# A graph network on one core: more edge cells and fewer fetched rows, TensorE's groups in pairs, and a sort without its pads

## The chip, the cores and the metric

The kernel runs on one core of one Trainium2 chip. The metric is the device time of one execution in microseconds (us). An execution is one launch of the whole program; the time given for a kernel is the median of several runs. One more execution is recorded by the hardware profiler, and everything that is said of single instructions comes from that one.

The engines are called by the profile's names: PE (TensorE, matrix products), PEld (its loading of weights), DVE (VectorE), ACT (ScalarE), POOL (GpSimd) and SP (SyncE, which here only issues transfers). POOL issues the indirect transfers, which gather rows of memory by a list of indices.

## The reference: what is computed

A graph has N = 12500 nodes with H = 128 features each and E = 200000 edges (src, dst), sorted by dst. Each edge has 16 attributes and one of 9 types. Four layers follow one another. In each, a node gathers the features of its neighbours, and a small dense network turns the sum into new features:

```python
# layer 0: a message for each edge, summed at dst, then a GRU cell
msg = h[src] @ W_msg.T + b_msg + edge_embed[edge_type]
messages = segment_sum(msg, dst)
x = layernorm(x + gru_cell(messages, x))
# layers 1 to 3 (GIN), summed at src
agg = segment_sum(join(x[dst], edge_attr @ enc_w + enc_b), src)
h = relu(batchnorm(agg @ w1 + b1)) @ w2 + b2
# after layer 3: x = layernorm(x + h)
```

`join` is a sum in layer 1 and a concatenation in layers 2 and 3. The kernel works on sums of features and sums of attributes, and lets the dense part apply the weights to the sums, so what costs time is the gather of 200000 rows by index and their sum by another index, four times.

## The kernel before, in words

**Data.** Nodes are cut into NB = 98 blocks of 128. A feature is kept as three bf16 pieces that add up to the float, so a node's row has H3 = 384 bf16 numbers. The rows of a layer's input lie in SBUF in tiles X of XC = 7 blocks each (14 tiles hold all 98 blocks), and in memory as `table`.

**Cells.** For each pair of an output block o and an input block b there is a cell of SL = 32 slots, which holds up to 32 edges between them (20.8 on average). Four cells are the 128 partitions of one tile of edges. PE gathers such a tile by four matmuls (L1550): a one-hot matrix `g` (128 nodes by 32 slots) picks the rows of block b out of X into PSUM tile `pg`. TG = 3 tiles are a group; `pg` is three PSUM banks wide and has two buffers. ACT copies a group to SBUF as bf16 (`e`, L1559); in layer 0, of every group with an even number k, ACT copies two thirds (L1556) and DVE one (L1557). PE then scatters: a matmul for each tile with the one-hot matrix `s` (128 edges by 128 nodes) adds the edges into the accumulator `acc` (L1507), which has one buffer of one bank.

**Fetched rows.** Layer 0 takes all 98 input blocks as cells: 25 tiles, nine groups. Layers 1 to 3 take only the first `ic` blocks as cells. The edges from the other blocks, and those beyond 32 in a cell, are put in lists, `rt` tiles of 128 edges for each o; POOL fetches their rows from `table` by one indirect transfer for each tile (L1484), and PE scatters them without a gather (L1515). Plan C (layer 1) has ic = 72 and rt = 5: 18 tiles, six groups. Plan D (layers 2 and 3) has ic = 60 and rt = 7: 15 tiles, five groups. Edges that find no place in either are added to memory tables `ovf` by a slow loop ahead of the layer. Fetched rows lie in those X tiles that the layer doesn't need for blocks, one whole X tile for each o; with 3 (layer 1) or 5 such tiles, o's rows are fetched two or four o's ahead.

**The loop** of `layer(i)` runs over o and, within it, over the groups k. Each step issues the gathers of group k, its copy, then the scatters of the group before (with one or two fetched rows), then one piece of other work: a tick of the dense part of a finished pair of blocks (`work`), and the one-hot matrices of the next o (`g` at L1471, four quarters of `s` at L1474). The scheduler may still reorder these within what the data allow. After the last scatter, `finish` adds the three pieces of `acc` into `s` by three DVE additions (L1527 to L1529), and every second o a dense part is queued (`gru` in layer 0, `gin` in the others: transposes L1415, two products L1424 and L1435, all through the one buffer of `psd`).

**Ahead of the layers** the cells' contents must be sorted. Two bitonic sorts of 128×2048 keys run on DVE, B (for attributes and their order) and A (for the cells). `sorter` (L284) runs levels 1 to 16 or 18; an exchange is a min and a max over all 2048 columns, halved between two instructions each (L299 to L322). From level 11 on PE transposes the keys (`turn`) and ACT copies them back. Of the 2048 columns EC = 1600 hold edges; the others hold one pad value. Beside sort B, PE, ACT and DVE count a histogram (`Sizes`).

**Attributes.** For each of the 98 blocks POOL fetches the attributes of its edges by 17 indirect transfers (L736); DVE and ACT prepare them and 17 matmuls add them up (L764). The generator `attributes` gives one step whenever it is asked. Beside sort A it is asked by this loop:

```python
            if at % 6 if at < len(plan) - 20 else done % ATTR:
                next(attr)
                done += 1
```

so at five of six exchanges, until 20 exchanges from the end, and from there only up to the end of a block. What is left is done in layer 0 (`pace`: after groups 1 and 5 of every o, and after group 3 of four o's in five) and in layer 1 (after group 3). When A's keys are stored (L787), POOL gathers the cells' slots in chunks of o's (L791), three of them at once ahead of the listing of the spilled edges, the others within layer 0.

Of the kernel before, what the change touches and what calls it, by code (L numbers as in the profile page):

```python
# [18 lines left out]
H = 128  # L19
# [31 lines left out]
IC = 72  # L51
CELL = 7
PLANS = (Plan("C", IC, 5, False, CELL + IC // 4), Plan("D", 60, CELL, True, 0))
RT = sum(p.rt for p in PLANS)
TW = CELL + IC // 4 + PLANS[0].rt
OV = 8
# [26 lines left out]
assert EP * EC == E and all(p.ic % (4 * TG) == 0 for p in PLANS)  # L83
# [5 lines left out]
def gnn_kernel(ctx: ExitStack, tc: tile.TileContext, x, xT, src, dst, ea, et, w_msg, w_ihT, w_hhT, b_msg,  # L89
# [35 lines left out]
    before = ctile([P, P], "before")  # L125
    V.tensor_scalar(before, diff, 0.0, None, op0=OP.is_gt)
    after = ctile([P, P], "after")
    V.tensor_scalar(after, diff, 0.0, None, op0=OP.is_lt)
    ident = diff
# [154 lines left out]
    def sorter(bufs, end):  # L284

        cur = 0

        def bits(t, c, cd):  # L290
# [4 lines left out]
            if cd == c + 1:  # L295
                v = t.rearrange("p (o r two i) -> p o r two i", two=2, r=2, i=1 << c)
                return [(v[:, :, r, 0, :], v[:, :, r, 1, :]) for r in range(2)]
# [3 lines left out]
        def exchange(c, first, cd, halved=False):  # L301
            nonlocal cur
            n = SC // 2
# [4 lines left out]
            else:  # L308
                exchanged(bufs[cur], bufs[1 - cur], c, first, cd)
# [75 lines left out]
    pre = ExitStack()  # L385
    pst = pre.enter_context(tc.tile_pool(name="pst", bufs=2, space=PSUM))
    pss = pre.enter_context(tc.tile_pool(name="pss", bufs=2, space=PSUM))
    kp = pre.enter_context(tc.tile_pool(name="keysA", bufs=1, side="right"))
# [28 lines left out]
    nc.scalar.dma_start(eti, by_part(et))  # L417
    for k in "BA":
        G.memset(keys[k][0], PADF)
        nc.scalar.dma_start(srt[k][:FRONT].rearrange("(p c) -> p c", p=P), keys[k][0][:, EC:EC + FRONT // P])  # L420
# [10 lines left out]
    def signed(k):  # L431
        odd = keys[k][0].rearrange("p (c two) -> p c two", two=2)[:, :, 1]
# [34 lines left out]
    nidentb = ctile([P, P], "nidentb", BF16)  # L467
# [277 lines left out]
    def add_up(b, at):  # L745
# [24 lines left out]
        yield  # L770
        own6 = owp.tile([P, 6, EA], BF16, name="own6")
        pieces6(own6, own, lambda a, b: own6[:, a:b, :], lambda t, n: t[:, None, :].to_broadcast([P, n, EA]))
        pt = psa.tile([P, 1024], BF16, name="acc") if early else psd.tile([P, 1024], BF16, name="d")
# [138 lines left out]
    class Listed:  # L912
# [24 lines left out]
        def mark(self, ahead):  # L937
# [55 lines left out]
            V.tensor_scalar(c[:, 1:2], self.most[:, 1:2], float(P - 1 - ahead * P), 0.0, op0=OP.add, op1=OP.max)  # L993
# [227 lines left out]
    eap = ctx.enter_context(tc.tile_pool(name="attrs", bufs=4))  # L1221
# [37 lines left out]
    with by_three():  # L1259
# [8 lines left out]
        while at < len(plan):  # L1268
            if at % 6 if at < len(plan) - 20 else done % ATTR:
                next(attr)  # L1270
                done += 1
# [14 lines left out]
        for c in range(3):  # L1286
            slots.gather(c)
        la = Listed()
        listing = la.mark(2)
# [4 lines left out]
        for _ in listing:  # L1294
            pass
    la.rest()
# [6 lines left out]
    ep = ctx.enter_context(tc.tile_pool(name="edges", bufs=3))  # L1303
# [346 lines left out]
```

## Time and profile before

| what | us |
|---|---|
| median of 3 runs | 5772.15 (5763.25 to 5779.61) |
| the profiled execution | 5775.41 |
| its span | 5773.6 |
| PE busy | 4590.5 (80%) |
| POOL busy | 3855.7 (67%) |
| DVE busy | 3500.1 (61%) |
| ACT busy | 3396.2 (59%) |
| weight loads busy | 2754.9 (48%) |

The busy time of an engine is the time in which it ran an instruction; issuing a transfer and waiting don't count. The shares are averages over stages that have different limits, and are to be read stage by stage: the page's second part cuts the span in 40 slices, and the trace can be asked for any stretch, for the waits of an engine in it, and for the timeline of single instructions. In a wait, "PE acc L1515 <- DMA x" means that PE's instruction of line 1515, which writes `acc`, could not start until a transfer into `x` had landed; the numbers behind it are the sum, the count and the longest one, in us. In a group of the page's fifth part the numbers are the busy time in us, the mean of one in ns, and the idle time of that engine just before such instructions with what ended it.

The whole program has 117175 instructions: 45358 matmuls, 9502 of DVE, 4901 of ACT and 3716 of POOL.

### The profile page before, as it was taken

How to read it: one execution, taken by the hardware profiler on the slowest of the kernel's cores; microseconds unless marked ns; L12 is line 12 of the kernel's file. 1: busy time of each engine (PE TensorE's matmuls, PEld its weight loads, DVE VectorE, ACT ScalarE, POOL GpSimd, SP SyncE). 2: the span in 40 equal slices, each digit the busy share in tenths (PEclk: the TensorE clock that was granted, in tenths of full speed). 3: DMA queues.
4: the chain of work that ended last, by engine and by line, in shares of the span. 5: the costliest groups of instructions: out<-in, count | busy, mean ns of one | idle time of the engine just before them, and what ended most of it. 6: DMA issues, size and time to landing. Idle time of an engine off the chain costs nothing. (4 is left out here: it accounts for less than half of the span.)

```text
span 5773.6 us, 117175 instructions
## 1 busy us (share of the span) xinstructions
PE 4590.5 (80%) x45358; PEld 2754.9 (48%) x45358; DVE 3500.1 (61%) x9502; ACT 3396.2 (59%) x4901; POOL 3855.7 (67%) x3716
## 2 busy tenths in 40 slices
PE   3874252118999999999799989988999997999998
PEld 3774122104444444444355555554555554555555
DVE  9987679837887777777444444443444443444444
ACT  7772131106666666666566666665666665666665
POOL 1001878866676767766677777775777776777776
PEclk9755555559999999999899999999999998999999
DMA  5101130012333333323444444445555555555554
GB/s 65 38 1 33 47 90 7 7 35 74 102 89 86 89 89 101 89 85 89 144 128 125 134 121 129 127 115 166 157 160 158 159 155 167 156 156 156 156 157 131
DMA packets 539973, 616.43 MB, mean 107 GB/s; under 512 B 130184, under 2 KB 458028, under 8 KB 538760
## 3 DMA queue, kind: packets, MB, share of 16 engines
q1 hardware_dynamic: 327302, 373.36, 20.1%
q0 software_dynamic: 148192, 202.82, 14.3%
q10 hardware_dynamic: 63914, 32.71, 2.7%
q8 instruction: 355, 5.82, 0.4%
q14 instruction: 210, 1.72, 0.1%
HBM read 519.72 MB, written 88.82 MB: 105 GB/s over the span
## 5 line engine op out<-in xcount | busy, mean ns | idle before, releaser
L1559 ACT CAST e<-g 128x1152 bf16<-128x1152 f32 (+1 forms) x2058 | 2216.2, 1091 | 907.7 <-PE g L1550 766.3
L1484 POOL DMA_INDIRECT x<-table,rowcol x1862 | 1861.2, 1000 | 641.4 <-issue 600.5
L736 POOL DMA_INDIRECT eat<-in_ea,eidcol x1666 | 1794.8, 1077 | 640.0 <-issue 495.0
L1550 PE MATMUL g<-x,g 128*32 128x384 bf16 x28420 | 1688.1, 333 | 93.6 <-DVE e L1557 54.2
L1507 PE MATMUL acc<-e,s 128*128 128x384 bf16 (+2 forms) x7154 | 1646.8, 344 | 116.9 <-ACT e L1556 51.6
L1507 PEld LDWEIGHTS <-s 128*128 128x128 bf16 (+1 forms) x7154 | 939.2, 153 | 745.4 <-issue 470.4
L1550 PEld LDWEIGHTS <-g 128*32 128x32 bf16 x28420 | 613.0, 96 | 911.6 <-issue 711.1
L1474 DVE TENSOR_TENSOR s<-iotas,outcol 128x704 bf16<-128x704 bf16 (+2 forms) x1568 | 838.7, 544 | 0.3 <-PE acc L1507 0.3
L1471 DVE TENSOR_SCALAR g<-inr,pidx 128x1920 bf16<-128x1920 bf16 (+2 forms) x392 | 329.9, 842 | 793.9 <-PE g L1550 685.7
L1515 PE MATMUL acc<-x,s 128*128 128x384 bf16 x1862 | 512.4, 335 | 155.5 <-DMA x<-table,rowcol 153.9
L1556 ACT CAST e<-g 128x768 bf16<-128x768 f32 x392 | 317.2, 809 | 192.9 <-PE g L1550 126.6
L567 PE MATMUL acc<-ot,oa 125*98 125x101 bf16 x1600 | 295.7, 358 | 126.8 <-ACT ot L548 95.6
L1527 DVE TENSOR_TENSOR s<-s,acc 128x128 f32<-128x128 f32 x392 | 112.5, 287 | 408.5 <-PE acc L1507 402.7
L1515 PEld LDWEIGHTS <-s 128*128 128x128 bf16 x1862 | 271.8, 146 | 176.1 <-issue 147.5
L567 PEld LDWEIGHTS <-oa 125*98 125x98 bf16 x1600 | 292.1, 277 | 129.6 <-issue 87.5
L548 ACT ACTIVATE ot<-dbb,bias 125x160 bf16<-125x160 bf16 (+2 forms) x1078 | 332.4, 406 | 16.4 <-PE acc L567 8.2
L800 POOL IOTA num<- 98x2176 uint16 x1 | 1.9, 1947 | 462.4 <-DMA sortedB<-keyB 462.4
L1427 ACT ACTIVATE gates<-d,shift,scale 128x256 f32<-128x256 f32 x294 | 150.1, 561 | 245.7 <-PE d L1425 245.7
L1557 DVE CAST e<-g 128x384 bf16<-128x384 f32 x392 | 216.6, 553 | 75.2 <-ACT e L1556 70.8
L1440 DVE TENSOR_TENSOR n<-d,b 128x256 f32<-128x256 f32 x98 | 41.6, 424 | 279.7 <-PE d L1435 278.6
L764 PEld LDWEIGHTS <-eoh 128*128 128x128 bf16 x1666 | 116.8, 163 | 197.3 <-DVE eoh L758 172.2
L316 DVE TENSOR_TENSOR keyA<-keyA 128x1024 f32<-128x1024 f32 (+1 forms) x178 | 190.9, 1072 | 15.4 <-ACT keyA L332 12.8
(423 smaller groups left out, 4761.8 us busy)
## 6 DMA issues: line engine op xcount, KB each, us to landing
inr<-inrow SPq DMA_DIRECT2D x196, 480.0 KB
inr<-inrow SPq DMA_DIRECT2D x98, 784.0 KB
inr<-inrow SPq DMA_DIRECT2D x98, 576.0 KB
x<-table,rowcol POOLq DMA_INDIRECT x1862
table<-x SPq DMA_DIRECT2D x147, 192.0 KB
eat<-in_ea,eidcol POOLq DMA_INDIRECT x1666
s<-ovf SPq DMA_DIRECT2D x147, 128.0 KB
ovf<-n SPq DMA_DIRECT2D x98, 128.0 KB
```

The lines of the kernel that those rows point to most:

```text
L548: A.activation(self.ot[j % 2][:, b, :ENDS[j] - c0], dbb[:, c0:ENDS[j]], AF.Sign, bias=self.bias[:, b:b + 1], scale=-1.0)
L567: T.matmul(cps[:NB, :NB + NQ - 1], self.oa[c // HC][:, :, c % HC], self.ot[j % 2][:, :, c - (ENDS[j - 1] if j else 0)], start=(c == 0), st ...
L736: G.indirect_dma_start(out=at[:, t, :], out_offset=None, in_=ea, in_offset=bass.IndirectOffsetOnAxis(ap=eidcol[:, b, t:t + 1], axis=0))
L1471: V.tensor_scalar(g[:, :nb * SL], inr[:, :nb * SL], pidx, None, op0=OP.is_equal)
L1474: V.tensor_tensor(st[:, f0:f0 + P // 4, :], iotas[:, f0:f0 + P // 4, :tw], outcol[a][:, o, None, c0:c0 + tw].to_broadcast([P, P // 4, tw]) ...
L1484: G.indirect_dma_start(out=t[:, j, :], out_offset=None, in_=tables[i], in_offset=bass.IndirectOffsetOnAxis(ap=rowcol[:, o, p.kept + j:p.ke ...
L1507: T.matmul(sums[o][:, :wid], st[:m, :, cell + t], e[:m, j, :wid], start=(t == 0), stop=(t == tiles - 1), skip_group_check=True)
L1515: T.matmul(sums[o][:, :H3], st[:, :, row + j], fetched[o][:, j, :], start=False, stop=False, skip_group_check=True)
L1550: T.matmul(pg[c * SL:(c + 1) * SL, j, :H3], g[:, b * SL:(b + 1) * SL], piece(X, b), start=True, stop=True)
L1556: A.copy(e[:, :2, :H3], pg[:, :2, :H3])
L1557: V.tensor_copy(e[:, 2, :H3], pg[:, 2, :H3])
L1559: A.copy(e[:m, :n, :H3], pg[:m, :n, :H3])
```

## The change

**Plans.** IC goes from 72 to 84. Plan C: ic = 84, rt = 3, so 21 tiles and seven groups. Plan D: ic = 72, rt = 5, so 18 tiles and six groups. CELL (where the cells start in the table of columns) 7 to 5, OV 8 to 12. Over the program this makes 31948 gather matmuls of 28420, 8036 scatters of 7154, and 1274 fetches with their matmuls of 1862.

**Rows.** The rows of an o no longer have an X tile of their own; rows fill the spare X tiles as a ring, so four o's have room in each plan and rows are fetched three o's ahead.

**Order in the layers.** PE's order is the one written (`manual_schedule`). Groups are taken in pairs: the gathers and copies of groups k and k+1, then the scatters of the pair before. `edges` has four buffers of 3. The split copy is now used in layers 1 to 3 as well, for odd k (in layer 0 for even k as before). `finish` reduces the three pieces of `acc` by one `tensor_reduce` and adds the result in SBUF. The dense parts yield once before their transposes and are queued after the pair.

**Sorts.** Exchanges of levels 1 to 8 leave out columns that hold only pads: 1600 columns at levels 1 to 6, 1664 and 1792 at levels 7 and 8. The memsets of the keys follow that.

**Attributes and cells.** Attributes are given out until 34 exchanges from the end (20 before), which leaves 16 early blocks of 18; in layer 0 after groups 1, 3 and 5 of every o; `attrs` has five buffers of 4. Two chunks of cells are gathered ahead of the listing and the third after it.

```diff
-IC = 72
-CELL = 7
-PLANS = (Plan("C", IC, 5, False, CELL + IC // 4), Plan("D", 60, CELL, True, 0))
+IC = 84
+CELL = 5
+PLANS = (Plan("C", IC, 3, False, CELL + IC // 4), Plan("D", 72, CELL, True, 0))
...
         def exchange(c, first, cd, halved=False):
             nonlocal cur
+            wide = min(SC, -(-EC // (1 << k)) << k)
...
-                exchanged(bufs[cur], bufs[1 - cur], c, first, cd)
+                exchanged(bufs[cur][:, :wide], bufs[1 - cur][:, :wide], c, first, cd)
...
-            if at % 6 if at < len(plan) - 20 else done % ATTR:
+            if at % 6 if at < len(plan) - 34 else done % ATTR:
...
-        for c in range(3):
+        for c in range(2):
             slots.gather(c)
         la = Listed()
-        listing = la.mark(2)
+        listing = la.mark(2, 2)
...
         for _ in listing:
             pass
+        slots.gather(2)
...
-        rb = NB // XC - xf
+        spare = [xpool.tile([P, XC, H3], BF16, name=f"x{k}") for k in range(xf, NB // XC)]
+        slots_of_rows = len(spare) * XC
+        rb = slots_of_rows // rt if rt else 1
...
+        def fetched(o, j):
+            return piece(spare, (o * rt + j) % slots_of_rows)
...
+        def add_group(o, st, e, k):
+            if k == 0:
+                sums[o] = psa.tile([P, 512], F32, name="acc")
+            if k == groups - 1:
+                scatter_rows(o, st, 2 * k - 2, rt)
             for j in range(min(TG, tiles - TG * k)):
...
+            if 0 < k < groups - 1:
+                scatter_rows(o, st, 2 * k - 2, 2 * k)
+            if k == groups - 1:
+                finish(o)
...
-            V.tensor_add(so[:, :H], so[:, :H], acc[:, 0:H])
-            V.tensor_add(so[:, :H], so[:, :H], acc[:, H:2 * H])
-            V.tensor_add(so[:, :H], so[:, :H], acc[:, 2 * H:H3])
+            whole = dq.tile([P, H], F32, name="whole")
+            V.tensor_reduce(whole, acc[:, :H3].rearrange("p (k f) -> p f k", k=3), axis=AX.X, op=OP.add)
...
+            V.tensor_add(so[:, :H], so[:, :H], whole)
...
-                if cells_only and n == TG and k % 2 == 0:
+                if n == TG and k % 2 != cells_only:
                     A.copy(e[:, :2, :H3], pg[:, :2, :H3])
                     V.tensor_copy(e[:, 2, :H3], pg[:, 2, :H3])
...
+                picked.append((o, st, e, k))
+                if k % 2 or k == groups - 1:
+                    work += fresh
+                    fresh.clear()
+                    for added_up in adding:
+                        ks = added_up[3]
+                        add_group(*added_up)
+                        tick()
+                        next(pieces, None)
...
+                        if pace(o, ks):
+                            next(attr, None)
+                    if k < 2:
+                        fetch(o + rb - 1)
+                    adding, picked = picked, []
...
-        layer(i, (lambda o, k: k in (1, 5) or k == 3 and o % 5, lambda o, k: k == 3)[i] if i < 2
-              else lambda o, k: False)
+        with tc.tile_pool(name="edges", bufs=4) as ep, tc.manual_schedule(engines={EN.PE}):
+            layer(i, (lambda o, k: k in (1, 3, 5), lambda o, k: k == 3)[i] if i < 2
+                  else lambda o, k: False, ep)
```

## The prediction

> **What bounds the kernel now.** I read the page's second part first, because the whole program has no single bound, only stages.
>
> ```profile
> PE   3874252118999999999799989988999997999998
> DVE  9987679837887777777444444443444443444444
> ACT  7772131106666666666566666665666665666665
> POOL 1001878866676767766677777775777776777776
> ```
>
> One digit is 144 us. Slices 1 to 8 are the two sorts: VectorE (DVE) is at 0.8 to 0.9, and GpSimd (POOL) joins in the fifth. From slice 9 TensorE (PE) stands at 0.9 or more, and POOL never falls below 0.6. The stages can be cut at SP's transfers: A's sorted keys are stored at 1162, layer 0 begins at 1205, layers 1, 2 and 3 at 2803, 3908 and 4844. The table of stretches then gives:
>
> ```profile
> 1205.00:2803.00 1598.00, 1405.29 (x14615) 705.63 (x14616) 1185.86 (x4549) 988.48 (x1459) 1101.74 (x1055) 0.96 0.32 89
> 2803.00:3908.00 1105.00, 990.69 (x10476) 580.62 (x10475) 494.58 (x1306) 738.15 (x856) 830.01 (x830) 0.96 0.43 127
> 3908.00:4844.00 936.00, 838.26 (x8884) 516.54 (x8884) 405.74 (x1050) 617.18 (x694) 688.54 (x686) 0.98 0.53 159
> 4844.00:5770.00 926.00, 845.41 (x8839) 512.64 (x8838) 433.28 (x1301) 587.89 (x605) 680.73 (x686) 0.98 0.52 153
> ```
>
> Columns: stretch, length, then PE, weight loads, DVE, ACT, POOL (busy, count), clock, DMA share, GB/s. Per block o (98 a layer), PE is busy 14.3, 10.11, 8.55 and 8.63 us. POOL looks free for a quarter of the time, and isn't: the costliest groups and layer 3's waits say why.
>
> ```profile
> L1484 POOL DMA_INDIRECT x<-table,rowcol x1862 | 1861.2, 1000 | 641.4 <-issue 600.5
> PE acc L1515 <- DMA x<-table,rowcol: 39.5, 37, 6.2
> ```
>
> Each fetch keeps POOL 1.00 us and is followed by about 0.30 of issuing, so 1.25 to 1.30 in all. Layer 1's 830 are then 1040 of 1105 us, layer 2's 686 are 858 of 936. PE waits for fetched rows 67 us in layer 1, 48 in layer 2, 39.5 in layer 3: POOL is a second bound, close behind PE. PE's own order is read in layer 3's timeline:
>
> ```profile
> 5206.32 1.21 PE L1550 MATMUL g<-x,g 128*32 128x384 bf16 x24
> 5208.04 1.20 PE L1507 MATMUL acc<-e,s 128*128 128x384 bf16 x6 [0.51 <-DVE s L1529]
> 5209.07 0.49 PE L1515 MATMUL acc<-x,s 128*128 128x384 bf16 x2
> 5209.49 0.67 PE L1550 MATMUL g<-x,g 128*32 128x384 bf16 x12
> 5210.09 0.71 PE L1507 MATMUL acc<-e,s 128*128 128x384 bf16 x3
> ```
>
> From start to start, 12 gathers take 0.605 and 24 take 1.155 to 1.21; three scatters take 0.55 to 0.58, six 1.04 to 1.12; a fetched row's matmul 0.21. The 0.51 is a scatter waiting until DVE's three additions have emptied the one accumulator.
>
> **The change, part by part**, against the profiled run (5775.4; span 5773.6, so 1.8 lie outside; 3.3 over the median).
>
> *Sorts.* One exchange is two DVE instructions of 1.22 = 2.44 us. Levels 1 to 8 (36 exchanges) leave out 448, 384 or 256 of 2048 columns: 21×0.219+7×0.1875+8×0.125 = 6.9 exchanges, 16.8 us a sort. In sort B, DVE is busy 99 of 100 us, but PE and ACT count the histogram beside it, so I take 10 (bounds 0 and 17). In sort A, DVE also waits for POOL's attribute transfers, full from 506 on; 5 (0 to 17). Two attribute blocks fewer before the end take some 3.6 us each of DVE out: 7.
>
> *Handover.* When A's keys are stored, POOL still has attribute transfers queued, and the cells' gather stands behind them:
>
> ```profile
> 1162.16 0.32 SPq L787 DMA_DIRECT2D sortedA<-keyA  x1
> 1195.60 0.94 POOL L736 DMA_INDIRECT eat<-in_ea,eidcol  x1 [0.30 <-issue]
> 1196.85 0.98 POOL L791 DMA_INDIRECT cells<-sortedA,start  x1 [0.31 <-issue]
> ```
>
> That is 34 us, 27 transfers. Stopping 14 exchanges earlier gives POOL some 14×2.44 = 34 us to empty its queue; I take 30. The third chunk's four cell transfers (1.27 each) move behind the listing: 5. Together 10+5+7+30+5 = −57 (bounds 0 and −75).
>
> *Layer 0.* Pairs of groups: two times three scatters (394 columns, 0.655 each) become six in 1.13, −0.18, four times an o; 24 gathers together save 0.05 a pair: −0.94 an o. PE waits 64 us in 1000 (65.4 o's), −0.98 an o, mostly for copies: with a fourth buffer of copies and six scatters between, most of it goes. It comes back in part, because the split copy is serial:
>
> ```profile
> 2013.43 0.80 ACT L1556 CAST e<-g 128x768 bf16<-128x768 f32 x1 [0.45 <-PE g L1550]
> 2014.27 0.56 DVE L1557 CAST e<-g 128x384 bf16<-128x384 f32 x1 [0.55 <-ACT e L1556]
> ```
>
> DVE's third starts only when ACT's two thirds are done, so a split copy ends 2.3 us after its gather's start (0.78+0.80+0.56 and gaps), where ACT's full copy (1.12) ends after 1.9. +0.8 after the odd ninth group, +0.4 where copies queue behind DVE's other work. Net −0.72×98 = −70. POOL's floor (about 980 attribute and 96 cell transfers ×1.25 to 1.3 = 1345 to 1400) lies under 1528. Bounds −150 and +30.
>
> *Layers 1 to 3, work.* Each o gets 12 gathers more, three scatters more, two rows fewer; pairing saves little here, since three plus three at 0.57 against six at 1.08 is 0.06. Layers 2 and 3: +0.52 gathers, +0.39 scatters (three pairs at 1.08 against five at 0.57), −0.42 rows = +0.49 us of PE an o; layer 1 the same to 0.05. The 588 fetches fewer free POOL (−588×1.25 = −735 us): layer 1 has some 685 left (860 us), layers 2 and 3 490 each (613). So the wait for rows goes. The ring of rows adds nothing on any engine; rows are fetched three o's ahead instead of two (layer 1) or four, a lead of 28 us at 9.3 an o, where layer 1 had 23. The accumulator's wait goes as well: one reduction of 128×384 replaces three additions (0.28 each, spread over 1.6 us by the one-hots between). No row shows it; by the sort's tensor_reduce of 2048 columns, 2.28, it is 0.43 to 0.5, and the next accumulation comes 24 gathers later. Bounds 0.3 (one addition's row) and 0.86 (three): both fit.
>
> *Layers 1 to 3, the new wait.* The order of after has, on every pair's second gather, a wait for DVE: its bank is emptied by the split copy. From the first gather's start: ACT's full copy from 0.78 to 1.90, ACT's two thirds to 2.71, DVE's third to 3.27. So 2.7 to 2.8 us must lie between the second gathers of two pairs; 1.2 of it are gathers, and the rest, scatters, rows and dense, must fill about 1.65. In layers 2 and 3, two o's have six such fillings: six scatters alone 1.12 (stall 0.53), six and two rows 1.46 (0.19), the other four over 1.7 (none). That is 0.36 an o. DVE adds to it when its third stands behind a reduction or a one-hot quarter (0.52 each): 0.24. Behind a waiting third stand the next reduction and one-hots, for which the next block's gathers and scatters wait. I take 0.6 an o, bounds 0 and 1.3, plus 0.1 for starts.
> Layer 1: 10.11+0.49+0.7 = 11.30×98 = 1107, +2. Layer 2: 8.55+0.49+0.7 = 9.74×98 = 955, +19. Layer 3: 8.63+0.49+0.7 = 9.82×98 = 962, +36. Larger loads (each inr 96 KB more, one or two more X tiles a layer) land ahead of use at a DMA share of 0.5; nothing.
>
> The Trainium skill ("PSUM — Partial Sum Buffer", Specifications) says ScalarE and VectorE can read PSUM at once when their banks differ. The row of the third above shows them one after the other. By the rule the second copy would be done some 0.56 sooner, most stalls would vanish, and the sum would be near the second rival's.
> The skill ("Trainium Kernel Development and Optimization", Best Practices) speaks against more cells: tiling "speeds up TensorE compute but NOT PSUM evacuation". By the rows, evacuation is 2.48 a pair, 7.4 an o against PE's 9.0 to 9.1: the sum keeps PE, the rule would make the copies the bound.
>
> **Sum.** −57−70+2+19+36 = −70, so 5775.4−70 = 5705; the median lies 3.3 lower, 5702, say 5700.
>
> **Rivals.**
> *Second, the copies keep up and only POOL was the gate.* For it: PE's waits for rows, 39 to 67 us a layer; ACT and DVE are half idle. Against: the serial third. Without the 0.6, layers 1 to 3 each lose 59 more, layer 0 the 0.8, 78 more; sorts −65: about −335, 5440.
> *Third, the sort's end is only moved.* Two attribute blocks' 34 transfers and the four of the cells go to layer 0, where POOL is 0.69 busy, some 0.85 with issuing. For it: POOL's queue is the same one. Each is 1.27, 38×1.27 = 48, so the first two parts give −79 instead of −127: 5750.
> *Fourth, slower: the wait for DVE's third is the bound in layers 1 to 3.* Place: every pair's second gather. For it: DVE runs the reduction, four one-hot quarters (2.2 us) and the dense additions in the same queue, and PE's order is now fixed by hand, so nothing fills a stall. Against: DVE is busy only 0.44 there. At 1.3 an o in place of 0.6: +0.7×294 = +206, 5905. It decides from 0.24 an o over my 0.6 (70/294): a mean stall of 0.84 makes the kernel no faster.
>
> **Numbers.** A measurement of this kernel can tell about 0.3%, 17 us. Forecast 0.45 (5620 to 5755); second 0.22; third 0.17, half of it within 17 us; fourth 0.16. Faster by over 0.3%: 0.45+0.22+0.07 = 0.74; within 0.10; slower 0.16. The range leaves out the lower part of the second and the upper of the fourth: 5510 to 5800.
>
> **What would show it.** The cells' first transfer right after A's store (handover under 15 us, not 34). Layer 0 near 1530. In layers 1 to 3, no wait of a row's matmul for its DMA, POOL's busy share near 0.5; a wait of the gathers for DVE's third, 35 to 60 us a layer. If that wait is under 15 us, the second rival; if over 80, the fourth. The forecast is wrong too if PE's busy time per o in layer 3 isn't 9.0 to 9.2.

## The result

The changed kernel is slower by 0.8%: median 5817.2 us (5813.1 to 5823.5), before 5774.3 (5763.3 to 5779.6), ratio 1.0078 with a 95% interval of 1.006 to 1.0095. The forecast was 5700, 1.3% less than before. Four runs of each kernel stand behind the result.

The whole hides parts of different signs. To see them, the span is cut at the same place of the program in both traces: where DVE first touches the finished sums of a block o (the first of its three additions before, L1527; the reduction after, L1549). Each term of the forecast stands beside the part that it falls in.

| part (profiled runs) | before | after | difference | forecast |
|---|---|---|---|---|
| start to layer 0's first block | 1317.8 | 1284.9 | -33 | -57 |
| to layer 0's last block | 1487.2 | 1526.8 | +40 | -70 |
| to layer 1's last block | 1110.2 | 1158.2 | +48 | +2 |
| to layer 2's last block | 932.1 | 923.0 | -9 | +19 |
| to the end | 926.3 | 918.4 | -8 | +36 |
| span | 5773.6 | 5811.3 | +38 | -70 |

So layers 0 and 1 lost, and layers 2 and 3, for which a loss was forecast, gained. The page of after, second part:

```profile
PE   3783342128888888888688888987999998999999
DVE  8987689747777777777555555555666665666666
POOL 1003878767677776777556565523555553655553
```

POOL's row has fallen from 0.7 to mostly 0.5 in the second half, as forecast, and PE's waits in layers 1 to 3 have no line left that names a fetched row: the fetches have ceased to be a bound. But PE's row stands at 0.8 from slice 10 to slice 25 (once at 0.6), where it was mostly 0.9 before. The next table is taken over 87 blocks of each layer, from the finish of o = 10 to that of o = 97, so that starts and ends stay out. Columns as in the prediction; before first, then after:

```profile
1466.00:2805.00 1339.00, 1237.85 (x12889) 622.93 (x12885) 1021.96 (x3908) 878.42 (x1299) 938.44 (x901) 0.99 0.33 93
2948.00:3915.00 967.00, 879.18 (x9332) 517.54 (x9324) 435.42 (x1141) 653.35 (x758) 727.54 (x728) 0.97 0.43 128
4041.00:4847.00 806.00, 731.49 (x7812) 451.81 (x7811) 355.17 (x913) 543.05 (x609) 610.43 (x607) 0.99 0.54 160
4970.00:5760.00 790.00, 736.33 (x7811) 449.15 (x7807) 382.29 (x1149) 518.94 (x532) 601.45 (x606) 0.99 0.52 154
```

```profile
1443.00:2812.00 1369.00, 1146.94 (x12921) 672.15 (x12921) 1029.66 (x3808) 858.10 (x1296) 1005.42 (x945) 0.97 0.32 89
2981.00:3970.00 989.00, 877.90 (x10407) 567.89 (x10400) 580.99 (x1297) 662.47 (x839) 502.80 (x485) 0.99 0.37 114
4099.00:4893.00 794.00, 762.35 (x8949) 518.05 (x8951) 500.17 (x1090) 543.74 (x695) 399.18 (x414) 1.00 0.48 148
5014.00:5800.00 786.00, 760.78 (x8938) 514.26 (x8930) 525.35 (x1324) 519.45 (x619) 404.61 (x415) 1.00 0.45 141
```

Read PE's busy time against the length. In layer 0 PE works 14.23 us an o before and 13.18 after: 1.05 less, where pairing was to save 0.94. Yet an o takes 15.73 in place of 15.38, so PE's idle time has grown from 1.16 to 2.55 an o. PE's waits in that stretch say for what, the longest two of before first, then those of after:

```profile
PE g L1550 <- DVE e L1557: 48.7, 72, 1.6
PE g L1550 <- ACT e L1559: 10.5, 15, 1.4
```

```profile
PE g L1572 <- DVE e L1579: 80.0, 105, 2.7
PE d L1386 <- DVE c L733: 33.2, 43, 2.4
PE d L784 <- DVE own L733: 24.5, 16, 2.3
PE d L771 <- DVE n L1404: 19.0, 17, 1.1
PE d L784 <- DVE n L1404: 18.5, 16, 1.7
PE g L1572 <- ACT e L1581: 12.2, 11, 1.5
PE d L784 <- ACT cT L1391: 10.9, 9, 3.0
```

The lines with `g` are gathers that wait for a copy, the first of them for DVE's third of a split one. All the others have `d` as the tile that PE wants to write: the one buffer of `psd`, which the GRU's transposes (L1386), the attributes' adding up (L771) and their transposes (L784) share. All waits at `d` together, with the shorter ones that aren't shown, are 129 us in 87 blocks, 1.48 an o; before they were 10 us, 0.12 an o. One place in the timeline shows how they come about:

```profile
2061.91 0.33 PE L1385 MATMUL d<-ident,s 128*128 128x128 f32 x1
2064.26 0.31 PE L1386 MATMUL d<-identb,c 128*60 128x128 bf16 x1 [2.02 <-DVE c L733]
2066.32 1.21 PE L771 MATMUL d<-attr,eoh 128*128 128x49 bf16 x17 [1.75 <-ACT cT L1391]
2067.45 2.11 PE L1572 MATMUL g<-x,g 128*32 128x384 bf16 x24
2069.50 1.75 PE L1534 MATMUL acc<-e,s 128*128 128x394 bf16 x6
```

PE waits for DVE's pieces, transposes, then waits until ACT has read that result out of `d`, because the attributes' matmuls come next in the written order and need the same buffer. The 24 gathers behind them need neither `d` nor the pieces, and the copies that empty their own banks had ended at 2061.8; yet they stand in the queue through 3.8 us of waiting.

In layers 2 and 3 the predicted wait is there, at about half of its predicted size: 0.36 and 0.27 us an o, where 0.6 was put into the sum. PE has no other wait in these stretches (layer 2, then layer 3):

```profile
PE g L1572 <- DVE e L1579: 31.6, 87, 0.5
PE g L1572 <- DVE e L1579: 23.8, 45, 0.9
```

One such wait in layer 3, with the rows of PE, ACT and DVE that bear on it:

```profile
5201.41 1.12 ACT L1581 CAST e<-g 128x1152 bf16<-128x1152 f32 x1 [1.10 <-PE g L1572]
5202.43 0.81 ACT L1578 CAST e<-g 128x768 bf16<-128x768 f32 x1
5202.97 0.56 DVE L1549 TENSOR_REDUCE whole<-acc 128x128 f32<-128x384 f32 x1 [2.06 <-PE acc L1534]
5203.44 0.55 DVE L1579 CAST e<-g 128x384 bf16<-128x384 f32 x1
5204.04 0.35 PE L1572 MATMUL g<-x,g 128*32 128x384 bf16 x4 [0.51 <-DVE e L1579]
```

The pair's gathers began at 5200.64. Full copy, two thirds, third: the third ends at 5203.99, 3.35 after the pair's start, and the next pair's second gather has waited 0.51 for it. The reduction stood ahead of the third, which began 0.2 us after ACT's part had ended.

### The profile page after: what moved, and what is told of

Same layout as the page of the kernel before. It is cut to its first block, busy times and chain, and to the rows that moved or that the text cites. A ratio compares the mean times of both kernels' runs of the same rounds, so it can differ in the third digit from the quotient of the medians.

```text
span 5811.3 us, 126172 instructions
## 1 busy us (share of the span) xinstructions
PE 4537.9 (78%) x49184; PEld 3011.8 (52%) x49184; DVE 3968.9 (68%) x9955; ACT 3390.3 (58%) x5190; POOL 3291.8 (57%) x3132
## 5 line engine op out<-in xcount | busy, mean ns | idle before, releaser
L1581 ACT CAST e<-g 128x1152 bf16<-128x1152 f32 (+1 forms) x1470 | 1582.9, 1077 | 739.1 <-PE g L1572 680.6
L1501 POOL DMA_INDIRECT x<-table,rowcol x1274 | 1255.5, 985 | 1232.3 <-PE acc L1523 498.6
L1534 PE MATMUL acc<-e,s 128*128 128x384 bf16 (+1 forms) x8036 | 1733.2, 342 | 0.8 <-DVE e L1579 0.4
L1534 PEld LDWEIGHTS <-s 128*128 128x128 bf16 x8036 | 1067.6, 151 | 566.2 <-issue 448.4
L1578 ACT CAST e<-g 128x768 bf16<-128x768 f32 x1274 | 1023.4, 803 | 335.1 <-PE g L1572 233.9
L1579 DVE CAST e<-g 128x384 bf16<-128x384 f32 x1274 | 703.3, 552 | 429.6 <-ACT e L1578 400.0
L1492 DVE TENSOR_TENSOR s<-iotas,outcol 128x832 bf16<-128x832 bf16 (+1 forms) x1568 | 831.6, 566 | 0.0
L1549 DVE TENSOR_REDUCE whole<-acc 128x128 f32<-128x384 f32 x392 | 217.3, 554 | 543.7 <-PE acc L1534 543.7
L1489 DVE TENSOR_SCALAR g<-inr,pidx 128x2304 bf16<-128x2304 bf16 (+2 forms) x392 | 357.1, 911 | 225.9 <-PE g L1572 225.4
L771 PEld LDWEIGHTS <-eoh 128*128 128x128 bf16 x1666 | 117.0, 163 | 220.3 <-DVE eoh L765 147.1
L1523 PEld LDWEIGHTS <-s 128*128 128x128 bf16 x1274 | 188.6, 148 | 20.9 <-issue 1.4
L321 DVE TENSOR_TENSOR keyA<-keyA 128x1024 f32<-128x1024 f32 (+4 forms) x178 | 185.4, 1042 | 17.2 <-ACT keyA L337 14.2
L322 DVE TENSOR_TENSOR keyA<-keyA 128x1024 f32<-128x1024 f32 (+4 forms) x178 | 184.6, 1037 | 0.0
```

Of the source, the lines that this page charges most:

```text
L1489: V.tensor_scalar(g[:, :nb * SL], inr[:, :nb * SL], pidx, None, op0=OP.is_equal)
L1492: V.tensor_tensor(st[:, f0:f0 + P // 4, :], iotas[:, f0:f0 + P // 4, :tw], outcol[a][:, o, None, c0:c0 + tw].to_broadcast([P, P // 4, tw]) ...
L1501: G.indirect_dma_start(out=fetched(o, j), out_offset=None, in_=tables[i], in_offset=bass.IndirectOffsetOnAxis(ap=rowcol[:, o, p.kept + j:p ...
L1523: T.matmul(sums[o][:, :H3], st[:, :, row + j], fetched(o, j), start=False, stop=False, skip_group_check=True)
L1534: T.matmul(sums[o][:, :wid], st[:m, :, cell + t], e[:m, j, :wid], start=(t == 0), stop=(t == tiles - 1), skip_group_check=True)
L1578: A.copy(e[:, :2, :H3], pg[:, :2, :H3])
```

## The experiments

Two causes were set against each other for the 88 us that layers 0 and 1 lost. **Theory 1**: PE's order, written by hand, puts PE behind the one buffer `d`, whose readers on DVE and ACT are late; the scheduler's order had put gathers and scatters in between. **Theory 2**: DVE's queue is late in itself, because a third of each split copy waits in it for ACT; whatever PE's order, something would wait. For layers 2 and 3 the question was which of the parts had gained: pairs, plans or fetches.

All kernels in one table, in us an o over the same 87 blocks, with the time of the profiled run. Where the text gives no interval, a kernel ran once; the kernel before took 5763 to 5788 us in the sets of runs that these come from.

| kernel | run | layer 0 | layer 1 | layer 2 | layer 3 |
|---|---|---|---|---|---|
| before | 5775 | 15.38 | 11.12 | 9.27 | 9.09 |
| after | 5813 | 15.73 | 11.37 | 9.13 | 9.03 |
| order free in layers 0, 1 | 5641 | 14.43 | 10.57 | 9.13 | 9.05 |
| all copies by ACT | 5641 | 15.25 | 10.90 | 8.70 | 8.70 |
| split on even k | 5689 | 15.81 | 10.81 | 8.71 | 8.65 |
| plans of before | 5799 | 15.87 | 10.98 | 9.15 | 9.30 |
| free in 0, 1 and even k | 5542 | 14.41 | 10.40 | 8.70 | 8.65 |
| free in all and even k | 5539 | 14.43 | 10.38 | 8.70 | 8.64 |
| stop at 20 | 5847 | 15.79 | 11.23 | 9.13 | 9.04 |
| one more yield | 5791 | 15.63 | 11.34 | 9.13 | 9.04 |
| before, order by hand | 6318 | 18.57 | 12.00 | 9.88 | 9.79 |
| before, short sort | 5767 | 15.36 | 11.17 | 9.25 | 9.09 |
| pairs undone | 6000 | 16.60 | 11.39 | 9.67 | 9.63 |
| other pace | 5573 | 14.00 | 11.62 | 8.70 | 8.67 |
| pace of 1.5 in layer 1 | 5470 | 13.97 | 10.50 | 8.70 | 8.67 |
| that, layer 0 by ACT | 5454 | 13.85 | 10.48 | 8.70 | 8.66 |

**PE's order left to the scheduler in layers 0 and 1.**

```diff
-        ... tc.manual_schedule(engines={EN.PE}):
+        ... (tc.manual_schedule(engines={EN.PE}) if i > 1 else ExitStack()):
```

> The changed kernel with PE's order left to the scheduler in layers 0 and 1, by hand only in layers 2 and 3. Theory 1 (the hand-written order puts PE behind the one dense buffer, whose readers on DVE are late; 1.5 us an o of such waits in layer 0, 0.3 in layer 1): layer 0 falls from 15.73 us an o to 14.5 to 15.0, layer 1 from 11.37 to about 11.1, the whole by 90 to 140 us to about 5690 to 5720. Theory 2 (DVE's queue is late whatever PE's order, because the split copy's third stands in it and waits for ACT): layer 0 stays within 0.3 of 15.73, the same idle time then stands at the gathers, the whole stays within 30 us of 5811.

Measured: 5641.2 against 5787.9 of before on the same chip; layer 0 at 14.43, layer 1 at 10.57. Layer 0's stretch and PE's longest waits in it:

```profile
1419.00:2674.00 1255.00, 1165.28 (x12928) 659.71 (x12927) 1020.74 (x3813) 857.52 (x1300) 966.25 (x909) 0.98 0.34 97
```

```profile
PE g L1572 <- DVE e L1579: 27.8, 66, 2.0
PE d L1399 <- DVE n L1404: 15.9, 2, 15.0
PE acc L1534 <- ACT e L1578: 12.7, 2, 12.5
```

All waits at `d` together have fallen from 129 to 25 us. PE's work is 13.39 an o, so 0.84 of the 1.05 saved is still there, and idle is 1.03. DVE does the same work as in after (1021 against 1030 us), in less time, so theory 2 by itself can't explain layer 0. Whether the other engines' orders changed with PE's isn't shown.

**All copies by ACT, in all layers** (the split's condition made false).

```diff
-                if n == TG and k % 2 != cells_only:
+                if False:
```

> The changed kernel with all copies of gathered groups made by ACT alone, in all four layers; DVE copies nothing. Theory 2 (DVE's third, and what stands behind it in DVE's queue, is what PE waits for): the gathers' waits for DVE's copies (80 us in layer 0, 75 in layer 1, 38 and 27 in layers 2 and 3) fall to a third, and waits for DVE's pieces at the dense buffer fall too: layer 0 at 14.9 an o or less, layer 1 at 10.8, layers 2 and 3 at 8.8 to 8.9; whole about 5640. Theory 1 (only PE's written order): layer 0 falls by less than 0.4 an o, as the waits at the dense buffer (1.5 an o) stay. A rival for layer 0: ACT, 10 us an o now and 11.2 then, becomes the engine that is late, and layer 0 doesn't move or gets slower.

Measured: 5640.5. Layers 2 and 3 fall by 0.43 and 0.33 an o, to a bound that is PE alone (756.00 us busy in 756.00 of layer 2), layer 1 by 0.47. Layer 0 falls by 0.48: its waits at `d` go from 129 to 94 us in 87 blocks, while the gathers' wait mostly changes its name, from 80 us for DVE and 12 for ACT to 79 for ACT. So DVE's third is what PE waited for in layers 1 to 3, and a smaller part in layer 0. The two theories were no rivals; each names a fault of its own. Whether DVE's third is late because of DVE's queue, as theory 2 has it, or because of its place in the pair, the next run tells.

**The split copy on even k in layers 1 to 3.**

```diff
-                if n == TG and k % 2 != cells_only:
+                if n == TG and k % 2 == 0:
```

> The changed kernel with the split copy on even k in layers 1 to 3 (layer 0 unchanged), so that in a pair the first group's copy is shared and the second is ACT's alone. If the length of the pair's copies is what counts (full, two thirds, third: 0.78+1.12+0.81+0.56 = 3.27 us after the pair's start, against 2.72 when ACT's two copies end the pair): the waits of the second gathers all but go, layer 1 falls from 11.37 to about 10.7 an o, layers 2 and 3 from 9.1 to about 8.8: whole 100 us less, about 5715. If DVE's queue is late by itself, the first gathers of the next pair wait in place of the second ones, and the layers stay within 0.15 an o.

Measured: 5688.8; layer 1 10.81, layers 2 and 3 8.71 and 8.65, near what the sum of the copies' lengths had (10.7 and 8.8). In layer 3 the wait for DVE's third falls from 23.8 to 6.5 us. The stretch, and the copies of one pair, whose gathers began at 5205.67:

```profile
4922.00:5675.00 753.00, 746.50 (x8939) 513.13 (x8938) 522.23 (x1323) 517.22 (x619) 459.67 (x420) 1.00 0.47 148
```

```profile
5206.39 0.80 ACT L1578 CAST e<-g 128x768 bf16<-128x768 f32 x1 [0.89 <-PE g L1572]
5207.09 1.12 ACT L1581 CAST e<-g 128x1152 bf16<-128x1152 f32 x1
5207.23 0.56 DVE L1579 CAST e<-g 128x384 bf16<-128x384 f32 x1 [0.45 <-ACT e L1578]
```

DVE still does its thirds (522 us busy, 525 in after), so it is not how much DVE does but where in the pair its turn comes. Full, two thirds, third is a chain of three; with the split first, ACT's second copy runs beside DVE's third, and the pair's copies end at 5208.21, 2.54 us after its start in place of 3.35.

**The plans of before in the changed kernel.**

```diff
-IC = 84
-CELL = 5
-PLANS = (Plan("C", IC, 3, ...), Plan("D", 72, ...))
+IC = 72
+CELL = 7
+PLANS = (Plan("C", IC, 5, ...), Plan("D", 60, ...))
...
-OV = 12
+OV = 8
```

> The changed kernel with the plans of before (72 and 60 blocks as cells, five and seven fetches an o, 1862 in all); ring, pairs, order, sorts and copies as changed. If the plans are worth little and the order made layers 2 and 3 faster: PE's busy time falls by 0.35 to 0.5 an o, layers 2 and 3 at 8.6 to 8.9 an o, layer 1 at about 11.0. If POOL's fetches held layers 2 and 3 of the kernel before: the waits of rows for their transfers come back (0.4 to 0.5 an o) and layers 2 and 3 stand at 9.1 to 9.3, layer 1 at 11.0 or more (1040 us of POOL's fetches alone are 10.6 an o). Layer 0 has the same edit in both and stays at 15.7.

Measured: 5798.6. PE's work falls by 0.45 an o in layer 3 (721 us in 87 blocks), but layer 3 takes 9.30, and layer 1 10.98. PE's waits in layer 3:

```profile
PE g L1572 <- DVE e L1579: 54.6, 84, 1.0
PE acc L1523 <- DMA x<-table,rowcol: 27.4, 31, 2.7
```

The rows' wait is back, and the copies' wait has doubled, likely because there is less work between two pairs. So the larger plans add some 0.5 us an o of PE's work, and pay for it in layer 3 (9.03 against 9.30), but not visibly in layer 2 (9.13 against 9.15). In layer 1 the old plan is the faster one while the order is by hand.

**Both faults mended** (order free in layers 0 and 1, split on even k).

> PE's order left to the scheduler in layers 0 and 1, and the split copy on even k in layers 1 to 3; once more, as the first run of it fell on a chip on which the kernel before took 8306 us. If the two faults are separate: layer 0 at 14.4 an o, layer 1 at 10.1 to 10.4, layers 2 and 3 at 8.65 to 8.75; whole about 5530, ratio to the kernel before 0.955 to 0.965. If layer 1's free order had hidden the copies already: layer 1 at 10.5, whole 5560.

Measured: 5543.6, ratio to before 0.9595 (0.9579 to 0.9611). Layer 0, which only the first edit touches, and layers 2 and 3, which only the second touches, stand where that edit alone had put them. In layer 1 the second is worth 0.17 an o once the order is free, where it was 0.56 by itself: the free order had hidden part of the copies.

**The same with the order free in all layers.**

> As the other, with PE's order left to the scheduler in all four layers; once more for the same reason. If the order by hand is bad wherever it stands: layers 2 and 3 below 8.65 an o. If it costs only where attribute work shares the dense buffer: layers 2 and 3 at 8.7 to 9.1; whole 0 to 80 us above the other.

Measured: 5538.8, layers 2 and 3 at 8.70 and 8.64, no different from 8.70 and 8.65. In the changed kernel the order by hand neither costs nor gains where no attribute work shares `d`.

**Attributes given out until 20 exchanges from the end.**

```diff
-            if at % 6 if at < len(plan) - 34 else done % ATTR:
+            if at % 6 if at < len(plan) - 20 else done % ATTR:
```

> The changed kernel with the attributes given out until 20 exchanges from the end; once more for the same reason. If the stop at 34 shortens the sort and POOL's queue: keys stored 5 to 10 us later than 1135.8, the cells' first transfer at about 1177 instead of 1154, layer 0's first block done about 20 us later and the whole at about 5830. If the work is only moved: whole within 10 us of the changed kernel's.

Measured: 5847.1. The keys are stored at 1144.7 (after: 1135.8) and the cells' first transfer comes at 1200.6 (after: 1154.2), 56 us behind the store. In POOL's timeline of this kernel, and then of after:

```profile
1199.38 0.94 POOL L743 DMA_INDIRECT eat<-in_ea,eidcol  x1 [0.30 <-issue]
1200.62 0.99 POOL L801 DMA_INDIRECT cells<-sortedA,start  x1 [0.31 <-issue]
```

```profile
1152.99 0.94 POOL L743 DMA_INDIRECT eat<-in_ea,eidcol  x1 [0.30 <-issue]
1154.24 0.99 POOL L801 DMA_INDIRECT cells<-sortedA,start  x1 [0.31 <-issue]
```

So the stop at 34 is worth 46 us at this place, of which some 30 us are left in the whole (34 against the profiled run of after, 30 against its median). Layer 0 gives nothing back for having two blocks of attributes fewer: 1527.1 us from its first block to its last, 1526.8 in after. Layer 1 is 15 us shorter, for which no cause was sought. So the third rival, a gain that is only moved, is refuted in this size. The queue is longer than the 34 us of the kernel before with the same stop: 425 attribute transfers come before the cells here, 408 in the kernel before, 391 in after. One block more, 17 transfers, is what a fifth buffer would allow POOL; the buffer was not tried by itself.

**One more yield ahead of layer 0's transposes.**

```diff
         yield
+        yield
         pt = psd.tile([P, 512], F32, name="d")
```

> The changed kernel with one more yield in layer 0's dense part between DVE's pieces and the transposes that read them; once more for the same reason. If closeness in the hand-written order makes PE wait: the transposes' waits for DVE's pieces (33 us in 87 o's) go and layer 0 falls by 0.3 an o or more. If DVE's queue is late by more than a pair: within 0.1.

Measured: 5790.7, layer 0 at 15.63. The transposes' wait for DVE's pieces is gone from the longest waits, as expected, but layer 0 has fallen by 0.1 and not by 0.3, as the second reading had it: others wait in its place, the GRU's first products 28 us for DVE, the attributes' transposes 31 instead of 25, the gathers 91 instead of 80. In one buffer, moving one user moves the wait.

These last four kernels had each run once before, on a chip on which the kernel before took 8306 us; they took 7140, 7164, 7465 and 7395 there, and no reading here rests on those runs.

**The kernel before, with PE's order by hand and nothing else.**

```diff
+        with tc.manual_schedule(engines={EN.PE}):
             layer(i, ...)
```

> The kernel before with one part of the change alone: PE's order as written in all four layers, no pairs. If the order by hand is the fault by itself: layer 0 rises from 15.38 to 16 or more an o, with PE's waits at the dense buffer, layer 1 from 11.12 by 0.2 or more, layers 2 and 3 by less than 0.2. If only pairs make it so (two ticks of other work three scatters apart): layer 0 stays within 0.3 of 15.38.

Measured: 6318.2. Layer 0 rises by 3.2 us an o, layer 1 by 0.9, and, against the expectation, layers 2 and 3 by 0.6 and 0.7. Layer 0's stretch and its longest waits:

```profile
1502.00:3118.00 1616.00, 1323.65 (x12874) 611.18 (x12866) 1046.05 (x3898) 882.50 (x1297) 901.64 (x893) 0.90 0.29 77
```

```profile
PE d L1369 <- DVE s L1529: 80.7, 43, 2.9
PE d L1372 <- DVE c L726: 59.3, 43, 2.2
PE acc L1507 <- DVE s L1531: 51.1, 27, 2.0
```

The order by hand costs time by itself; no pairs are needed for it. Here the transposes (L1369) and the next accumulation (L1507) wait for DVE's additions of the finished sums. In after these are one reduction, and the transposes come a yield later; that this is why the order did less harm there is likely, and was not tried by itself.

**The kernel before with the short exchanges alone** (the sort's hunks of the change).

> The kernel before with the shortened exchanges alone. By the prediction: B's keys stored 10 us earlier than 505.9 (bounds 0 and 17), A's 15 us earlier than 1162.2 (0 to 34); POOL's queue of attribute transfers behind it stays at 34 us or grows; the layers don't move; whole about 15 us less. If DVE isn't what the sorts wait for, the whole stays within 5 us.

Measured: 5767.3. B's keys are stored 7.4 us earlier (498.5), A's 14.2 (1148.0); the cells' first transfer 14.2 (1182.6). The whole is 8 us below the profiled run of before, where 15 were expected; single runs of before differ by as much.

**The pairs undone.**

```diff
-                if k % 2 or k == groups - 1:
+                if True:
...
-                    if k < 2:
+                    if k == 0:
                         fetch(o + rb - 1)
```

> The changed kernel with its pairs undone (gathers of a group, then the scatters of the one before), order by hand kept. PE's busy time in layer 0 rises by 0.9 to 1.05 an o in any case. If the order by hand alone is the fault, the idle time stays at 2.5 an o, layer 0 at 16.6. If it is the pairs (two ticks close together, two copies in a row), the idle time falls to 1.2 and layer 0 stands at 15.4 to 15.6; layers 2 and 3 then lose their waits for DVE's third, but pay for the changes between gathers and scatters: 9.0 to 9.3.

Measured: 5999.8; layer 0 16.60 as the first reading had it (PE's work 14.30 in place of 13.18, idle 2.3). Layers 2 and 3 stand at 9.67 and 9.63, above both readings, and there PE does nothing but work:

```profile
5146.00:5984.00 838.00, 827.78 (x8952) 469.94 (x8951) 536.15 (x1324) 539.93 (x620) 428.07 (x414) 1.00 0.43 133
```

827.78 against 760.78 in after for the same matmuls: pairs save 0.77 us an o in layer 3.

**Attributes moved from layer 0 to layer 1.** With both faults mended, PE stands still 65 us at the start of layer 1 while POOL works off attribute transfers. So the pace was changed:

```diff
-layer(i, (lambda o, k: k in (1, 3, 5), lambda o, k: k == 3)[i] ...
+layer(i, (lambda o, k: k in (1, 5) or k == 3 and o % 5, lambda o, k: k in (1, 5))[i] ...
```

> The faster version (PE's order free in layers 0 and 1, split copy on even k in layers 1 to 3) with the pace of attributes lowered in layer 0 to that of the kernel before (2.8 steps an o, not 3) and raised to two steps an o in layer 1. In the faster version PE and ACT stand still 55 to 65 us at the start of layer 1, while POOL issues attribute transfers that are left over from layer 0, and layer 1's spilled edges stand behind them. If layer 0 has become bound by POOL: some 66 transfers fewer there, 82 us of POOL, the stand goes, layer 0's blocks stay at 14.4 an o, layer 1 rises by 0.2 an o at most; whole about 5500. If that stand has another cause: whole within 15 us of 5544.

Measured: 5574.7, ratio 0.9649 (0.9636 to 0.9662), so slower than without it. The stand fell from 65 to 22 us and layer 0 to 14.00, but layer 1 rose to 11.62, with 12.67 in its first third. There PE waited for rows again:

```profile
PE acc L1523 <- DMA x<-table,rowcol: 76.9, 18, 9.0
```

**The same with one and a half steps in layer 1** (`k == 3 or k == 5 and o % 2`).

> PE's order free in layers 0 and 1, split copy on even k in layers 1 to 3, layer 0's attributes at 2.8 steps an o, and layer 1's at 1.5 steps an o in place of 2. With two steps POOL had (3 + 6.8) x 1.25 = 12.3 us of transfers an o at the start of layer 1, where 12.67 was measured, and PE waited 77 us for fetched rows; with 1.5 it has (3 + 5.1) x 1.25 = 10.1. If POOL was the bound there: layer 1 at 10.4 to 10.6, layer 0 at 14.0, the stand at the start of layer 1 stays near 20 us, whole about 5470 to 5490. If the attributes' adding up on PE and DVE was what cost layer 1: 11.2 or more, whole 5540.

Measured: 5468.0, ratio 0.9463 (0.945 to 0.9476), 2 us under the expected range: layer 1 10.50, as the reading with POOL as the bound had it, and its wait for rows falls from 77 to 11 us. This is the fastest version with an interval, 5.4% below the kernel before.

**And layer 0's copies by ACT.**

> As the other, and in layer 0 all copies by ACT. In layer 0 the gathers wait 28 us for DVE's third and 12 for ACT; if the serial third costs layer 0 as it cost layers 1 to 3, layer 0 falls from 14.0 to 13.7 an o; if ACT's longer copies take its place (ACT 10 us an o, then 11.2), layer 0 stays at 14.0 or rises.

Measured in one run: 5454.0. Layer 0 falls by 0.12 an o to 13.85, less than half of the 0.3 that the first reading had.

## Why the prediction was wrong

*Sorts and handover, -57 forecast, -33 measured.* The short exchanges gave 14.2 of 15. The stop at 34 was sized by the exchanges' time (34 us of POOL's queue, 30 taken), and the queue fell by 16: from 34.7 us behind the store to 18.4. With the changed kernel's buffers the stop itself is worth 37 us (55.9 to 18.4), near what it was sized at. The fifth buffer, which the prediction did not price, is the likely reason for the longer queue (425 transfers against 408 at the same stop; 17 at 1.25 are 21 us, and 55.9 less 34.7 is 21.2). The cells' first transfer comes 42.6 us earlier; another 10 are lost before the first block ends. PE's longest waits there are 46.0 us (L1121) and 53.7 us (L654) in after, 62.2 (L1110) and 45.5 (L1507) before; which of them cost the 10 was not tried.

*Layer 0, -70 forecast, +40 measured: the step that failed.* The pairing's gain was right (0.94 an o forecast, 1.05 measured). The prediction took 0.98 an o of waits away and put 1.2 in their place, all of it for copies: 0.8 for the split copy and "+0.4 where copies queue behind DVE's other work". That came out near, 1.06 at the gathers. What failed is that the sum has no term at all for PE's waits at `d`: it put the hand-written order at nothing in layers 0 and 1. Measured: 1.48 an o at `d`, where it had been 0.12. The text had said of PE's order that it "is now fixed by hand, so nothing fills a stall", but only in the fourth rival, for layers 1 to 3, and had not counted who shares `d` in layers 0 and 1. The free order gives back 1.3 us an o, takes the waits at `d` from 129 to 25 us, and puts layer 0 at 14.43, near the 14.66 that 15.38 less the forecast's 0.72 would be. The order by hand alone adds 3.2 to the kernel before. So this step is shown.

*Layer 1, +2 forecast, +48 measured.* In part the same step: 0.31 an o at `d`, for which there was no term, and 0.86 at the gathers, together 1.2 where 0.6 was taken. PE's work rose by nothing (10.09 against 10.11 an o) where 0.49 was forecast, since the pairs paid for the cells (with the pairs undone it is 10.86). 27 of the 48 us lie in the first eleven blocks. 17 attribute transfers at 2833 to 2854 stand ahead of the layer's first row there, while ACT waits until 2856; how much of the 27 they cost was not tried.

*Layers 2 and 3, +19 and +36 forecast, -9 and -8 measured.* Two terms were mis-sized. That "pairing saves little here", 0.06 a pair, was read from the kernel before, whose three scatters have fetched rows ahead of them or behind. Between gathers, as in the timeline of the kernel without pairs, twelve gathers take 0.605 and three scatters 0.65 from start to start; in pairs it is 1.09 and 1.13. That is 0.29 a pair, 0.87 an o, and 0.77 is measured. So PE's work rose by 0.35 and 0.28 and not by 0.49. And the wait for DVE's third was 0.36 and 0.27, not 0.6: the part that came from the fillings' lengths was right in layer 2 (0.36), and the 0.24 added for DVE's queue was not needed. By the prediction's own signs, PE's busy time in layer 3 was to be 9.0 to 9.2 an o, and is 8.74; the wait for DVE's third was to be 35 to 60 us a layer, and is 75, 32 and 24 in 87 blocks.

*The rivals.* The fourth, slower, was right in its sign and only partly in its place. The gathers' wait that it names is 0.86 an o in layer 1, 0.36 and 0.27 in layers 2 and 3; their mean, 0.50, stays under the 0.84 at which that rival decides. The largest wait stood at the dense buffer in layer 0, which it doesn't name. The second was right that the copies could keep up, though not as written: with the split on even k, layers 2 and 3 stand at 8.7, 0.4 to 0.6 below before.

ScalarE and VectorE do read PSUM at once here, as the Trainium skill ("PSUM — Partial Sum Buffer", Specifications) says they can: in the rows of the even run above ACT's full copy and DVE's third run side by side from 5207.23 to 5207.79, each from a buffer of its own. In after, 628 of the 1274 thirds overlap a full copy of ACT. The third never overlaps the two thirds of its own group: in all 1274 it starts 0.03 us or more after them, and the trace has it waiting for ACT's `e`, the tile that both write. So the two in sequence, which the prediction set against the page, are an order that the program keeps and no sign of what PSUM allows.

The other page's words ("Trainium Kernel Development and Optimization", Best Practices) are "TensorE tiling speeds up compute but not PSUM evacuation"; that this speaks against more cells is the prediction's own reading. It did not bind: with all copies by ACT, PE is busy 754 of 757 us in layer 3.

Three readings of the page were too round, though nothing in the sum rests on them. PE's row of before stands at 0.7 or 0.8 in seven of its last 31 slices, POOL's falls to 0.5 once, and DVE's lies between 0.6 and 0.9 in the sorts.

## What to carry to other kernels

Fixing an engine's order by hand is a cost of its own, to be priced wherever a buffer with one copy is shared: list for each instruction in that order who must have emptied its tile, and what of the queue behind it could have run meanwhile. A change of shape that saves work (here pairs, 1.05 us an o) can be bought back by such a queue and be invisible in the total; PE's busy time and idle time have to be read separately, stage by stage. In a pair of copies, share the first and not the second where the shared one's parts run one after the other, as here: the last one to finish sets the next pair's start.

## What the runs showed of the hardware

The stalls cost more than their length, because PE's granted clock falls. In after around the place shown above:

```profile
2062.00:2067.00 5.00, 1.23 (x14) 0.98 (x15) 3.42 (x12) 1.89 (x5) 3.79 (x4) 0.68 0.80 249
2063.00:2063.50 0.50, 0.00 (x0) 0.00 (x0) 0.50 (x3) 0.26 (x1) 0.24 (x1) 1.00 1.05 389
2063.50:2064.00 0.50, 0.00 (x0) 0.00 (x0) 0.50 (x2) 0.15 (x1) 0.46 (x1) 0.83 0.88 360
2067.00:2070.00 3.00, 3.00 (x35) 1.53 (x34) 2.64 (x9) 1.56 (x3) 2.38 (x3) 0.50 0.33 79
```

The clock falls to half at 2063.83, when PE has stood still for 1.6 us, and is whole again at 2070.66. The second wait, of 1.75 us, comes only after the fall. At half the clock 24 gathers take 2.11 us in place of 1.09 to 1.16. In the 3.41 us ahead of the fall PE had worked 1.82 us. The 19 falls in this stretch of after are all of this kind: each spell at half lasts 3.41 or 6.83 us, and in the 3.41 us ahead of it PE had worked 0.7 to 2.0 us, with no pause over 2.7. In layer 0's stretch the clock stood at half for 26 us in the kernel before, 75 us in after, and 332 us in the kernel before with its order by hand, whose mean granted clock of 0.90 the fence of that experiment shows. The Trainium skill ("TensorE: Matmul & The Clock Gate", What's actually happening) puts the fall after an idle window of some 3.4 us; here windows of that length in which PE was busy for up to 2.0 us were enough.
